# Added matmuls in the pauses of TensorE, in layer 2 of a four-layer kernel

## The chip, the cores and the metric

The kernel runs on one core of a Trainium2 chip. The metric is the device time of one execution in microseconds (us), as the median of several runs. Of the core's engines these matter here: TensorE (PE in the profile, its weight loads PEld) multiplies matrices into PSUM; VectorE (DVE) and ScalarE (ACT) work element by element; GpSimd (POOL) gathers and scatters rows by indirect DMA; SyncE (SP) issues most other DMAs.

## What is computed

`x` is 32 sequences of 64 rows of 256 float32 numbers, 2048 rows in all. Four layers follow one another, each with a mixing part and a feed-forward part, and each adds its result to `x`. The change lies in layer 2. Its mixing part is a recurrence over the 64 steps of a sequence, and its feed-forward part lets each of 8 experts choose its 512 best rows:

```python
xW = jnp.einsum('ntd,dh->nth', x, Wx) + b
def step(prev_h, xw_t):
    next_h = jnp.tanh(xw_t + prev_h @ Wh)
    return (next_h, next_h)
_, hs = jax.lax.scan(step, h0, jnp.swapaxes(xW, 0, 1))
...
k = max(MIN_CAPACITY, ceil(N * CAPACITY_FACTOR / E))
scores = jax.nn.softmax(xt @ Wr, axis=-1)
G, idx = jax.lax.top_k(scores.T, k)
X_in = xt[idx]
h = jax.nn.gelu(jnp.einsum('ekd,edh->ekh', X_in, W1) + b1[:, None, :], approximate=False)
X_e = jnp.einsum('ekh,ehd->ekd', h, W2) + b2[:, None, :]
contrib = (G[..., None] * X_e).reshape(E * k, D)
out = jnp.zeros((N, D), dtype=x.dtype).at[idx.reshape(-1)].add(contrib)
```

Here `h0` is the conditioning input, `xt` is the recurrence's output by rows, and `N` is 2048.

## The kernel before

The four layers run one after another. Layers 0 to 2 share one set of pools: `bank()` gives one of four PSUM tiles of 128x512, `wide()` one of two of 128x1024. Layer 3 opens its own PSUM pool after these are closed. The code is traced in program order; a scheduler then gives each engine its own instructions in an order, taking among those that it reckons ready the one traced first. Each engine runs its list in order, and waits on semaphores for the others. A float32 matmul shows as two records of PE and two weight loads, a transpose as one.

Layer 2 has these stages.

- **Recurrence** (`layer2`). XT holds the input transposed, HT the states transposed. `feed(s)` puts the input projection of step s into PSUM (8 matmuls through `add`, line 1111, with Wx; at every eighth step also the bias, line 1101, into a new bank). `add(s, wh, ...)` adds the product of the state before with Wh (8 matmuls, also line 1111, 16 records). ScalarE takes tanh (line 1131), VectorE transposes the new state (line 1132), and the next step's product needs that. Between them TensorE can do only what doesn't depend on the new state: `feed(s + 4)`, and at every fourth step `route(s - 1)`, two matmuls (line 1123, four records) that put the router's logits into the first 128 columns of the wide tile `lg`. Its other half, columns 512 on, isn't used. `feed` calls may run further ahead than four steps, as far as the four banks go.
- **Scores.** After the last `route`, VectorE copies the logits (line 1145), softmax follows, and TensorE transposes the scores (line 1185).
- **Search** (`top_tokens`). 15 rounds find each expert's 512th score, two bits a round. In each, VectorE counts the scores above three trial values (line 1200), one small matmul adds the counts up by expert (line 1203), and VectorE picks the next trials (lines 1207 to 1211). Then TensorE transposes the result (line 1213), and some prefix sums settle ties (lines 1223, 328 to 330).
- **Slots** (`slots`, with `by_position=True` only here). `positions` makes prefix sums with two matmuls (lines 300, 301). VectorE builds index arithmetic and, for each expert, a 128x2048 one-hot tile (line 345); TensorE multiplies it into the list of row numbers, 16 matmuls of float16 per expert (line 385). Expert 0's list goes out first, so that GpSimd can gather its rows (line 452) while the other lists are made.
- **Experts** (`routed`). For each expert, the gathered rows are transposed (line 459), the hidden layer is 16 matmuls of 128x128 by 128x512 (line 426) and the output 32 matmuls (line 435).

Of the kernel before, what the change touches and what calls it, by code (L numbers as in the profile page):

```python
# [20 lines left out]
P = 128  # L21
NB = 32
NS = 64
N = NB * NS
NT = N // P
# [4 lines left out]
NE = 8  # L30
# [40 lines left out]
class Kernel:  # L71
# [34 lines left out]
    def evacuate(self, out, in_):  # L106

        self.turn += 1
        if self.turn % 2:
            self.nc.scalar.copy(out, in_)  # L110
        else:
            self.nc.vector.tensor_copy(out, in_)

    def row_broadcast(self, pool, name, row, width, parts=P, tag=None, engine=None):

# [178 lines left out]
    def positions(self, pool, flags, ne, name):  # L294

        nc = self.nc
        off = self.scanned(pool, flags, ne, name)
        ps = self.bank()
        pos = ps[:, :ne * NT].rearrange("p (e t) -> p e t", t=NT)
        nc.tensor.matmul(pos, self.before, flags[:, :, 1:], start=True, stop=False)  # L300
        nc.tensor.matmul(pos, self.ones, off, start=False, stop=True)
        return pos

    def count_sequences(self, pool, flags):
# [43 lines left out]
    def slots(self, pool, flags, capacity, name, by_position=False):  # L348

        nc = self.nc
        nchunk = -(-capacity // P)
        full = [P, NE, NT]
        sel = flags[:, :, 1:]
        pos = self.positions(pool, flags, NE, "sl")
        other = pool.tile(full, F32, name="sl_other")
        nc.vector.tensor_scalar(other, sel, -1.0, 1.0, ALU.mult, ALU.add)

        nc.vector.scalar_tensor_tensor(other, pos, float(capacity), other, ALU.is_ge, ALU.max)  # L360
        key = pool.tile(full, I32, name="sl_key")
        nc.vector.scalar_tensor_tensor(key, other, float(N), pos, ALU.mult, ALU.add)
        part_i = pool.tile(full, I32, name="sl_part_i")
        nc.vector.tensor_scalar(part_i, key, P - 1, None, ALU.bitwise_and)
        part = pool.tile(full, F16, name="sl_part")
        nc.vector.tensor_copy(part, part_i)
        chunk = pool.tile(full, I32, name="sl_chunk")
        nc.vector.tensor_scalar(chunk, key, 7, None, ALU.logical_shift_right)

        give = pool.tile([P, NE, NT, nchunk], F16, name="sl_give")  # L370
        indices = []
        ohs = self.one_hots()

        for e0, e1 in ((0, 1), (1, NE)):
            ne = e1 - e0
            ps = self.bank()
            for c in range(nchunk):
                nc.vector.scalar_tensor_tensor(give[:, e0:e1, :, c], chunk[:, e0:e1], float(c),
                                               self.number.unsqueeze(1).to_broadcast([P, ne, NT]),
                                               ALU.is_equal, ALU.mult)  # L380
            for e in range(e0, e1):
                oh = self.one_hot(ohs, e, part)
                at = (e - e0) * nchunk
                for t in range(NT):
                    nc.tensor.matmul(ps[:, at:at + nchunk], oh[:, :, t], give[:, e, t],
                                     start=(t == 0), stop=(t == NT - 1))
            n = ne * nchunk
            read = self.cp.tile([P, n], I32, name=f"{name}_read{e0}")
            nc.scalar.activation(read, ps[:, :n], AF.Relu, bias=self.minus)  # L389
            add = self.cp.tile([P, n], I32, name=f"{name}_add{e0}")  # L390
            if by_position:

                nc.vector.tensor_scalar(add, read, NB - 1, NS.bit_length() - 1, ALU.bitwise_and,
                                        ALU.logical_shift_left)
                nc.vector.scalar_tensor_tensor(add, read, NB.bit_length() - 1, add, ALU.logical_shift_right,
                                               ALU.bitwise_or)
                empty = pool.tile([P, n], I32, name=f"sl_empty{e0}")
                nc.vector.tensor_scalar(empty, ps[:, :n], 0.5, self.spare, ALU.is_lt, ALU.mult)
                nc.vector.tensor_tensor(add, add, empty, ALU.bitwise_or)
            else:  # L400
                empty = pool.tile([P, n], F32, name=f"sl_empty{e0}")
                nc.vector.tensor_scalar(empty, ps[:, :n], 0.5, self.spare1, ALU.is_lt, ALU.mult)
                nc.vector.scalar_tensor_tensor(add, ps[:, :n], -1.0, empty, ALU.add, ALU.add)
            indices += [(read[:, i:i + 1], add[:, i:i + 1]) for i in range(n)]
        return indices, nchunk
# [663 lines left out]
    def layer2(self, weights):  # L1069
        nc, tc, I = self.nc, self.tc, self.I  # L1070
# [3 lines left out]
        XT = self.xp.tile([P, DC, NS, NB], F32, name="XT", tag="XT")  # L1074
        both = P // NS
        for t in range(NT):
            ps = self.bank()
# [6 lines left out]
        HT = self.xp.tile([P, DC, NS, NB], F32, name="HT", tag="CT")  # L1084
# [5 lines left out]
        with tc.tile_pool(name="l2r", bufs=1) as rp:  # L1090
            wx, wh, b, ones, wr = weights
            width = DC * NB
            steps = 512 // width
            into = {}

            def feed(s):

                if s % steps == 0:
                    into[s // steps] = ps = self.bank()
                    for q in range(QG):  # L1100
                        nc.tensor.matmul(
                            ps[q * NB:(q + 1) * NB].rearrange("p (s x) -> p s x", x=width), ones,
                            b[:, q].rearrange("p m f -> p (m f)").unsqueeze(1).to_broadcast([3 * NB, steps, width]),
                            start=True, stop=True)
                add(s, wx, lambda c: XT[:, c, s])

            def add(s, w, state):
                at = s % steps * width
                for c in range(DC):
                    for q in range(QG):  # L1110
                        nc.tensor.matmul(into[s // steps][q * NB:(q + 1) * NB, at:at + width], state(c),  # L1111
                                         w[:, c, q].rearrange("p m f -> p (m f)"), start=False,
                                         stop=True, skip_group_check=True)

            lead = 4
            lg = self.wide()
            rows = table[:, :D].rearrange("(s b) d -> b s d", b=NB)

            def route(s):

                t = s // 4
                for c in range(DC):
                    nc.tensor.matmul(lg[:, t * NE:(t + 1) * NE], HT[:, c, s - 3:s + 1].rearrange("p s b -> p (s b)"),  # L1123
                                     wr[:, c], start=(c == 0), stop=(c == DC - 1))

            for s in range(lead):
                feed(s)
            for s in range(NS):
                add(s, wh, lambda c: self.condT[:, c, :] if s == 0 else HT[:, c, s - 1])
                at = s % steps * width  # L1130
                nc.scalar.activation(H[:, s], into[s // steps][:, at:at + width], AF.Tanh)
                nc.vector.transpose(HT[:, :, s], H[:, s].rearrange("p (m f) -> p m f", f=NB))
                if s % 4 == 0 and s:
                    route(s - 1)
                if s + lead < NS:
                    feed(s + lead)
                if s % 16 == 15:
                    for q in range(QG):
                        for m in range(DC):
                            f = m * P + q * NB  # L1140
                            nc.sync.dma_start(rows[:, s - 15:s + 1, f:f + NB],
                                              H[q * NB:(q + 1) * NB, s - 15:s + 1, m * NB:(m + 1) * NB])
            route(NS - 1)
            logits = rp.tile([P, NT, NE], F32, name="r2_l")
            nc.vector.tensor_copy(logits.rearrange("p t e -> p (t e)"), lg[:, :NT * NE])
            score = rp.tile([P, NT, NE], F32, name="score")
            self.softmax(rp, score, logits, [P, NT, NE])
            nc.scalar.dma_start(table[:, D:].rearrange("(t p) e -> p t e", p=P), score)
            k = max(4, math.ceil(N * 2.0 / NE))
            self.top_tokens(rp, flags, score, k)  # L1150
# [8 lines left out]
    def top_tokens(self, pool, flags, scores, k):  # L1159
# [6 lines left out]
        m = 2  # L1166
# [31 lines left out]
        for i, shift in enumerate(shifts):  # L1198
# [1 line left out]
                nc.vector.tensor_scalar(seen, by, trial.bitcast(F32)[:, j:j + 1], 0.0, ALU.is_ge, ALU.add,  # L1200
                                        accum_out=cnt[:, j:j + 1])
            ps = self.bank()
            nc.tensor.matmul(ps[:, :J], members, cnt, start=True, stop=True)
            more = i + 1 < len(shifts)
            if more:
                nc.vector.tensor_tensor(base, tries[:, i + 1], kth.to_broadcast([P, J]), ALU.bitwise_or)
# [754 lines left out]
```

## Time and profile before

| | us |
|---|---|
| median of 3 runs | 1902.01 (1901.94 to 1907.29) |
| the profiled execution, its own time | 1906.38 |
| its span, first to last instruction | 1904.7 |
| mean granted TensorE clock over the span | 0.866 of full speed |
| recurrence, first tanh to last | 942.57 to 1029.71 |
| scores, last `route` to the transpose of line 1185 | 1030.27 to 1033.66 |
| search, first count to the transpose of line 1213 | 1035.75 to 1070.72 |
| slots, from there to the first expert's line 426 | 1070.72 to 1096.27 |

A time in the profile is in us from the span's start. A group line gives the engine, its line in the kernel, the operation, the tile written and the tiles read, how often, and in brackets how long the engine stood idle before and who ended that. The granted clock is the share of full speed at which TensorE was let run; a stage's mean can lie between the steps of 0.5 and 1.0 that single stretches show.

### The profile page before, as it was taken

How to read it: one execution, taken by the hardware profiler on the slowest of the kernel's cores; microseconds unless marked ns; L12 is line 12 of the kernel's file. 1: busy time of each engine (PE TensorE's matmuls, PEld its weight loads, DVE VectorE, ACT ScalarE, POOL GpSimd, SP SyncE). 2: the span in 40 equal slices, each digit the busy share in tenths (PEclk: the TensorE clock that was granted, in tenths of full speed). 3: DMA queues.
4: the chain of work that ended last, by engine and by line, in shares of the span. 5: the costliest groups of instructions: out<-in, count | busy, mean ns of one | idle time of the engine just before them, and what ended most of it. 6: DMA issues, size and time to landing. Idle time of an engine off the chain costs nothing.

```text
span 1904.7 us, 26705 instructions
## 1 busy us (share of the span) xinstructions
PE 1548.1 (81%) x9935; PEld 1193.5 (63%) x9935; DVE 713.6 (37%) x2357; ACT 599.6 (31%) x1306; POOL 576.0 (30%) x740
## 2 busy tenths in 40 slices
PE   6699998999996939999675499999665768778777
PEld 5467766888885728888564356667543546546455
DVE  3594033111111161111213601001356668787775
ACT  2222332333331203333211032222134455545443
POOL 0244310233320013332100133331235445555452
PEclk8699998999997959999885599999866778788789
DMA  7454541566632045666511044442300100101000
GB/s 255 125 167 129 141 122 59 162 182 181 190 96 88 6 157 158 191 177 169 150 26 25 12 117 127 106 112 64 114 31 22 41 22 23 32 14 32 14 12 12
DMA packets 158406, 183.81 MB, mean 97 GB/s; under 512 B 37540, under 2 KB 137536, under 8 KB 158272
## 3 DMA queue, kind: packets, MB, share of 16 engines
q1 hardware_dynamic: 123920, 143.34, 23.7%
q0 software_dynamic: 21248, 29.24, 8.9%
q10 hardware_dynamic: 13104, 9.47, 1.6%
q8 instruction: 81, 1.33, 0.3%
q14 instruction: 53, 0.43, 0.1%
HBM read 152.22 MB, written 29.79 MB: 96 GB/s over the span
## 4 chain that ended last, share of the span: by engine, by line
PE 27%; DVE 8%; POOL 6%; issue 5%; ACT 4%; DMA 1%; SPq 0%; POOLq 0%; DVEq 0%; ACTq 0%
PE bank L426 6%; PE bank L435 6%; PE bank L1111 3%; PE bank L1740 2%; PE bank L1856 2%; PE bank L1663 1%; PE bank L1873 1%; PE bank L1437 1%; ACT squares L1582 1%; PE bank L1798 1%; PE bank L1575 1%; POOL mag L1332 1%; PE wide L1123 1%; PE bank L1774 1%; POOL mb_root L147 1%
## 5 line engine op out<-in xcount | busy, mean ns | idle before, releaser
L435 PE MATMUL bank<-w,hidden 128*128 128x256 f32 (+1 forms) x2080 | 458.7, 379 | 0.0
L435 PEld LDWEIGHTS bank<-w,hidden 128*128 128x128 f32 (+1 forms) x2080 | 387.8, 187 | 66.2 <-issue 6.5
L426 PE MATMUL bank<-xeT,w 128*128 128x256 f32 (+2 forms) x1440 | 398.5, 436 | 25.9 <-ACT xeT L110 20.5
L426 PEld LDWEIGHTS bank<-xeT,w 128*128 128x128 f32 x1440 | 274.7, 193 | 137.1 <-issue 63.4
L469 POOL DMA_INDIRECT acc<-y,l_add x56 | 89.2, 1594 | 254.8 <-ACT y L468 146.1
L603 DVE TENSOR_TENSOR y<-bank,b 128x256 f32<-128x256 f32 x58 | 24.6, 425 | 360.8 <-PE bank L435 360.8
L428 ACT ACTIVATE hidden<-bank,ge_cols 128x256 f32<-128x256 f32 x232 | 109.8, 473 | 114.9 <-PE bank L426 114.9
L452 POOL DMA_INDIRECT xg<-table,l_read x56 | 71.7, 1280 | 244.9 <-ACT l_read L389 164.9
L467 DVE TENSOR_TENSOR y<-bank,b 128x256 f32<-128x256 f32 (+1 forms) x56 | 23.5, 420 | 297.7 <-PE bank L435 297.6
L428 ACT ACTIVATE hidden<-bank,bias_cols_b 128x256 f32<-128x256 f32 (+1 forms) x128 | 73.7, 580 | 120.6 <-PE bank L426 119.6
L605 POOL DMA_INDIRECT acc_c<-y,pl_add x30 | 47.8, 1594 | 137.0 <-DVE gate L595 98.6
L605 POOL DMA_INDIRECT acc<-y,pl_add x28 | 44.6, 1592 | 131.7 <-DVE gate L595 93.5
L1856 PE MATMUL bank<-wg,yT 128*128 128x352 f32 x128 | 58.2, 586 | 15.3 <-ACT h_glu L1858 7.2
L1663 PE MATMUL bank<-wqkv,mo_uT 128*128 128x512 f32 (+1 forms) x128 | 57.2, 602 | 15.9 <-ACT ex L1727 13.3
L468 ACT ACTIVATE y<-y,xg 128x256 f32<-128x256 f32 (+1 forms) x56 | 28.4, 508 | 128.7 <-DVE y L467 128.7
L1873 PE MATMUL bank<-wd,hT 128*128 128x256 f32 x192 | 62.1, 465 | 6.1 <-ACT hT L1577 2.9
L426 PE MATMUL bank<-XT,w 128*128 128x256 f32 x256 | 65.0, 409 | 2.0 <-DVE C L899 1.3
L110 ACT COPY xeT<-bank 128x256 f32<-128x256 f32 (+1 forms) x57 | 20.6, 362 | 143.7 <-PE bank L124 88.0
L604 ACT ACTIVATE y<-y,gate 128x256 f32<-128x256 f32 x58 | 29.5, 509 | 106.9 <-DVE y L603 106.9
L1856 PE MATMUL bank<-wu,yT 128*128 128x352 f32 x128 | 54.0, 546 | 9.9 <-DVE h_glu L1860 9.1
L591 POOL DMA_INDIRECT xg<-table_x,pl_read x30 | 31.9, 1062 | 99.1 <-DVE pl_empty L544 57.5
L426 PEld LDWEIGHTS bank<-XT,w 128*128 128x128 f32 x256 | 51.0, 205 | 9.6 <-DVE C L899 1.4
(581 smaller groups left out, 2391.6 us busy)
## 6 DMA issues: line engine op xcount, KB each, us to landing
w<-in_L_ffn_W_dram SPq DMA_DIRECT2D x44, 1024.0 KB
w<-in_L_cond_ew_dram SPq DMA_DIRECT2D x30, 1024.0 KB
w<-in_L_ffn_w_dram SPq DMA_DIRECT2D x16, 1024.0 KB
ad<-ada SPq DMA_DIRECT2D x64, 128.0 KB
X<-acc SPq DMA_DIRECT2D x12, 512.0 KB
w<-in_L_cond_sw_dram SPq DMA_DIRECT2D x4, 1024.0 KB
ad<-ada SPq DMA_DIRECT2D x64, 64.0 KB
b<-in_L_ffn_b_dram SPq DMA_DIRECT2D x30, 128.0 KB
```

Source lines behind the costliest of these rows:

```text
L426: nc.tensor.matmul(ps[:, :cols], w1[:, c, f * P:(f + 1) * P], xT[:, c, :], start=(c == 0), stop=(c == DC - 1))
L428: nc.scalar.activation(h[:, f, :cols], ps[:, :cols], func, bias=bias[:, f:f + 1])
L435: self.nc.tensor.matmul(ps[:rows, :D], h[:, f, at:at + rows], w2[:, f, :], start=(f == 0), stop=(f == FC - 1))
L452: nc.gpsimd.indirect_dma_start(out=xg[:rows], out_offset=None, in_=table, in_offset=bass.IndirectOffsetOnAxis(ap=indices[e * nchunk + c][0 ...
L469: nc.gpsimd.indirect_dma_start(out=acc, out_offset=bass.IndirectOffsetOnAxis(ap=indices[e * nchunk + c][1][:rows], axis=0), in_=y[:rows], ...
L591: nc.gpsimd.indirect_dma_start(out=xg, out_offset=None, in_=table, in_offset=bass.IndirectOffsetOnAxis(ap=read[:, c:c + 1], axis=0), bound ...
L605: nc.gpsimd.indirect_dma_start(out=acc, out_offset=bass.IndirectOffsetOnAxis(ap=add[:, c:c + 1], axis=0), in_=y, in_offset=None, bounds_ch ...
L1111: nc.tensor.matmul(into[s // steps][q * NB:(q + 1) * NB, at:at + width], state(c), w[:, c, q].rearrange("p m f -> p (m f)"), start=False, ...
L1663: nc.tensor.matmul(ps[:, :hi - lo], uT[:, j, c], K["wqkv"][:, c, lo:hi], start=(c == 0), stop=(c == DC - 1))
L1740: nc.tensor.matmul(ps[rows, h * (HD + 1):(h + 1) * (HD + 1)], ex[rows, r, j * DC + c, odd], V[rows, j, h], start=True, stop=True)
L1856: nc.tensor.matmul(ps[:, :half], yT[:, c], w[:, c, cols], start=(c == 0), stop=(c == DC - 1))
L1873: nc.tensor.matmul(ps[:, :D], hT[:rows, k], self.wd[:rows, k], start=(k == 0), stop=(k == KC - 1))
```

## The change

A new helper, `repeat`, issues n float32 matmuls of the identity (128x128) with the first `width` columns of XT into the unused half of `lg`, which nothing reads. `issue_after(mark)` puts them behind a given instruction in TensorE's order; they wait for nothing else. It is called with width 128 once per step of the recurrence, and with width 512 otherwise: 5 after the last `route`, 3 after each of the 15 counts, 4 after the slots' prefix sums, 3 after expert 0's one-hot products and 1 after each of experts 1, 2 and 3. That is 64 matmuls of 128 columns and 60 of 512. The computed result doesn't depend on them.

```diff
+    def repeat(self, mark, n, width=P):
+
+        with self.tc.issue_after(mark):
+            for _ in range(n):
+                self.nc.tensor.matmul(self.unread[:, :width], self.ident, self.any_rows[:, :width], start=True,
+                                      stop=True)
+
...
-        nc.tensor.matmul(pos, self.ones, off, start=False, stop=True)
+        self.last_count = nc.tensor.matmul(pos, self.ones, off, start=False, stop=True).ins
...
         pos = self.positions(pool, flags, NE, "sl")
+        if by_position:
+            self.repeat(self.last_count, 4, 512)
...
-                    nc.tensor.matmul(ps[:, at:at + nchunk], oh[:, :, t], give[:, e, t],
-                                     start=(t == 0), stop=(t == NT - 1))
+                    last = nc.tensor.matmul(ps[:, at:at + nchunk], oh[:, :, t], give[:, e, t],
+                                            start=(t == 0), stop=(t == NT - 1))
+                if by_position and e < 4:
+                    self.repeat(last.ins, 1 if e else 3, 512)
...
             lg = self.wide()
+            self.unread = lg[:, 512:]
+            self.any_rows = XT.rearrange("p c s b -> p (c s b)")
...
-                add(s, wh, lambda c: self.condT[:, c, :] if s == 0 else HT[:, c, s - 1])
+                mark = add(s, wh, lambda c: self.condT[:, c, :] if s == 0 else HT[:, c, s - 1])
...
                 if s + lead < NS:
                     feed(s + lead)
+                self.repeat(mark, 1)
...
-            route(NS - 1)
+            self.repeat(route(NS - 1), 5, 512)
...
-            nc.tensor.matmul(ps[:, :J], members, cnt, start=True, stop=True)
+            self.repeat(nc.tensor.matmul(ps[:, :J], members, cnt, start=True, stop=True).ins, 3, 512)
```

`add` and `route` return their last matmul for this.

## The prediction

> **What bounds the kernel now.** I read the page first, then busy time by stage, then stretches of 3.41 us, then single instructions in order of time.
>
> ```profile
> PE 1548.1 (81%) x9935; PEld 1193.5 (63%) x9935; DVE 713.6 (37%) x2357; ACT 599.6 (31%) x1306; POOL 576.0 (30%) x740
> ...
> PEclk8699998999997959999885599999866778788789
> ```
>
> TensorE carries most of the span. A slice of the second line is 47.6 us; slices 21 and 22, counted from 0 (1000 to 1095 us), have half the clock. They are the end of layer 2's recurrence, its search and its slots. Busy time in those stages (columns: PE, PEld, DVE, ACT, POOL, granted clock, DMA share, GB/s):
>
> ```profile
> 942.57:1029.93 87.36, 65.50 (x2047) 53.47 (x2039) 15.45 (x63) 14.28 (x64) 0.00 (x0) 0.74 0.22 50
> 1034.50:1070.40 35.90, 8.73 (x30) 7.51 (x30) 23.90 (x176) 0.00 (x0) 0.00 (x0) 0.50 0.05 5
> 1076.53:1079.24 2.71, 0.00 (x1) 0.00 (x1) 2.60 (x11) 0.00 (x0) 0.00 (x0) 0.50 0.00 0
> 1079.24:1096.27 17.03, 10.73 (x137) 9.57 (x137) 10.30 (x17) 1.01 (x3) 7.05 (x4) 0.50 0.12 33
> ```
>
> They are the recurrence, the 15 rounds of the search, the pause after the slots' prefix sums, and the one-hot products. The clock is 0.74 in the first and 0.50 in the rest. In stretches of 3.41 us:
>
> ```profile
> 992.27:995.68 3.41, 2.66 (x118) 2.17 (x106) 0.74 (x3) 0.67 (x3) 0.00 (x0) 1.00 0.06 11
> 995.68:999.10 3.42, 2.12 (x79) 1.55 (x68) 0.74 (x3) 0.67 (x3) 0.00 (x0) 0.98 0.00 0
> 999.10:1002.51 3.41, 2.44 (x76) 1.96 (x80) 0.73 (x3) 0.67 (x3) 0.00 (x0) 0.50 0.02 5
> ```
>
> A stretch with 79 matmul records is followed by half clock; one with 118 is not. So filling does matter here. What a step costs is seen in the distance between ScalarE's tanh's (full clock, then half clock, steps without a projection):
>
> ```profile
> 995.87 0.22 ACT L1131 ACTIVATE H<-bank 128x64 f32<-128x64 f32 x1 [0.83 <-PE bank L1111]
> 996.93 0.22 ACT L1131 ACTIVATE H<-bank 128x64 f32<-128x64 f32 x1 [0.83 <-PE bank L1111]
> ...
> 1006.20 0.22 ACT L1131 ACTIVATE H<-bank 128x64 f32<-128x64 f32 x1 [1.06 <-PE bank L1111]
> 1007.48 0.22 ACT L1131 ACTIVATE H<-bank 128x64 f32<-128x64 f32 x1 [1.05 <-PE bank L1111]
> ```
>
> 1.06 against 1.28 us: half clock costs 0.22 us a step. One round of the search, at half clock:
>
> ```profile
> 1043.08 0.59 PE L1203 MATMUL bank<-tk_cnt,tk_members 128*128 128x3 f32 x2 [1.81 <-DVE tk_seen L1200]
> 1043.71 0.16 DVE L1207 TENSOR_SCALAR_CACHE_REDUCE tk_enough<-bank 128x3 f32<-128x3 f32 x1 [0.68 <-PE bank L1203]
> ...
> 1045.48 0.59 PE L1203 MATMUL bank<-tk_cnt,tk_members 128*128 128x3 f32 x2 [1.81 <-DVE tk_seen L1200]
> ```
>
> The period is 2.40 us, of which TensorE works 0.59 and pauses 1.81; VectorE bounds it. The price of a repeated matmul, from the chain of work of a later expert:
>
> ```profile
> 1128.10 13.97 PE bank L426 x32
> ```
>
> That line is 16 matmuls of 128x128 by 128x512 in float32, each in two records (32): 13.97/16 = 0.873 us each at clock 1.00. The added ones have this very shape and type.
>
> **The change, part by part.** It removes nothing, moves no DMA, and touches neither SP's nor POOL's queue. It adds matmuls on TensorE, which runs them in order; each stands behind a named matmul and waits for nothing. What is queued behind them on TensorE is the next recurrent product, the next count L1203, the transposes L1185 and L1213, and the one-hot products L385; VectorE and ScalarE wait for all of these. The extra hold on XT and on lg's second half costs nothing: no later tile uses either name, and the PSUM pool is closed only at layer 3, after the last repeat. That cover would be gone only if layer 3 came before the slots.
>
> 1. Recurrence, 64 repeats of 128x128 by 128x128: a quarter of 0.873 us, so 0.21 each at full clock, 0.43 at half. The gain first: steps 8 to 24, nearly all at full clock, took 956.04 to 976.43 = 20.4 us, 10.2 for eight steps. Steps 8 to 63 took 73.7 us (956.04 to 1029.71); at 10.2 for eight they'd take 70.1, saving 3.6. Steps 2 to 8, partly at half clock, save about 1.3. Together 4.9. The cost: the 16 recurrent records take 0.27 us to issue, so a step of 1.06 leaves 0.79; two input projections (0.28 each) and a repeat fill 0.77, so the repeat hides. In the 16 steps that also hold the router's four records (0.54 us) TensorE is the bound already (0.54+0.56+0.27 = 1.37, and 956.04 to 957.41 is 1.37), so 16 x 0.21 = 3.4 is added. Net -1.5. Bounds: -4.9 (router steps find room) and +4 (the clock still drops, and a repeat costs 0.43 where it doesn't fit).
> 2. After the last router product, 5 repeats of 512: 5 x 0.873 = 4.37. L1185 starts 3.39 us after that product starts (1030.27, 1033.66) because of softmax. After: 0.54 + 4.37 = 4.91, so +1.5; the transpose's own 0.15 is saved: +1.35. If the clock is half at first, up to +4.5.
> 3. Search, 3 repeats in each of 15 rounds. 3 x 0.873 = 2.62 us must pass through a pause of 1.81. The count itself at full clock is 0.27 (two records at 0.135, a quarter of the router's 0.54), and the first repeat's weights load after it, about 0.06 to 0.13. The period is 2.62+0.27+0.06 = 2.95 us, bound by TensorE. The last round's repeats also stand before L1213. From the first count to L1213 it was 34.97 us (1035.75 to 1070.72); it becomes 15 x 2.95 = 44.3: +9.3. Bounds: +8.4 at 2.89 a round, +10.3 at 3.02. That the count gets 0.26 faster is in the 2.95 and buys nothing beyond.
> 4. L1213 to the second prefix sum's end, 5.81 us with 3.82 of PE at half clock: at most half of that, 1.9, is saved if the clock stays, and I reckon 1.5, since what follows the last column of each doesn't shrink; PE is busy under half the time there, like the stretches that dropped. I take -0.8 (0 to -1.5).
> 5. 4 repeats behind the prefix sums: 3.49 us at full clock, 6.98 at half, in a pause of 2.71. +0.8 to +4.3; the clock may have dropped in part 4 and must be won back: +1.9.
> 6. Slots' one-hot products: 3 repeats behind expert 0's, 1 behind each of experts 1 to 3. The first 16 records take 1.16 and gain 0.3 to 0.5, an estimate with half of it as its limit. Those after experts 0 to 2 lie in the wait for the gathers (TensorE idles for L459 until 1090.83). The one behind expert 3 does not: after 1090.83 TensorE works without a pause up to the first expert's L426. +0.9 to +1.75 there. If full clock lasted to 1091, the other products would gain 2.5. Net +1.2 (-3 to +3). The first L426 run took 16.36 us against 13.97, 2.4 lost to half clock; a wait of over 5 us for gathers precedes it still, so I leave it at 0 (±2.4).
>
> Sum: -1.5 +1.35 +9.3 -0.8 +1.9 +1.2 = +11.5 us. The profiled execution took 1906.4 us (span 1904.7 and 1.7 around it), 4.4 above the median of 1902.0; I put the same sum on both: 1917.9 for a profiled one, 1913.5 for the median.
>
> Two rules of the Trainium skill bear on this, both on the page TensorE: Matmul & The Clock Gate. The section Back-to-back issue gap gives a warm 512-column matmul about 216 ns. By that, three repeats are 0.65 us and vanish in 1.81; the search would only gain, about 15 x 0.26 = 3.9. By the row they are 2.62. The row has the shape and the float32 of this edit, so it decides. The section Why this matters for your kernels asks only for no idle gap above about 3 us to stay warm. By that, the search, with pauses of 1.8, would be at full clock already and the repeats could buy nothing: without the gains of parts 1 and 4 the sum is about +17. The rows speak against it: 0.50 all through the search.
>
> **Rivals.**
> - Repeats fit and clock gains remain (faster). The place is the search; it is decided by a 512 repeat costing at most 0.6 us (a round without repeats is 2.40-0.26 = 2.14 at full clock, less 0.3 for the count, by 3). Then: recurrence -4.9, counts -3.9, part 4 -1.5, one-hots -2.5, first L426 -2.4: -15, 1887 us. The clock rows speak for it, the 0.873 against. 0.08.
> - Balance (within 0.3%): search as reckoned, but router steps take the repeat for nothing (-4.9), and the slots stay at full clock to 1091 with the first L426 (-3.6, -2.4): near +1 to +4, 1904 us. For it: TensorE will be full for 45 us before. Against: the waits for gathers. 0.18.
> - Repeats cost and the clock doesn't hold in the recurrence and slots (slower still): +4, +4.5, +9.3, +4.3, +3 = +25, 1927 us. For it: 79 records were too few, and steps without projections get only two more records. Against: those two stream four times the columns of eight small ones. 0.10.
> - TensorE becomes the bound of the search and the rest about cancels: 1913.5 us. 0.64.
>
> **How the numbers follow.** About 0.3%, 5.7 us, is what a measurement of this kernel can tell from no change. Most of the likeliest case and all of the third lie above 1907.7: slower 0.73; balance and the low edge of the likeliest: same 0.19; faster 0.08. The range 1901 to 1923 takes in the balance and leaves out the first rival and the outer part of the third. The likeliest case's own range is 1907 to 1921.
>
> **What would show it.** In the profile after: 3 repeats as 6 records between counts, the period 2.9 to 3.0 us, PE near 100% busy with clock 1.00 there, and VectorE's L1200 no longer what the count waits for. L1185 starts about 4.9 us after the last router product, L1213 44 us after the first count. In the recurrence the clock is near 1.0 and tanh's are 1.06 apart, about 1.58 at router steps. It is wrong if a 512 repeat takes under 0.6 us, if the search's round is below 2.4, or if the recurrence shrinks by more than 5.

## The result, and the profile after

The changed kernel took 1908.34 us in the median of 12 runs (1904.01 to 1913.79), the kernel before 1904.10 in 12 runs beside it (1901.73 to 1910.35): ratio 1.0026, 95% interval 1.0016 to 1.0036. So it is slower by 4 to 5 us, clear of the noise but less than half of the 11.5 that were forecast. 1908.3 lies in the range of 1901 to 1923. The difference of 0.26% is inside the 0.3% that the prediction called no change, to which it gave 0.19, against 0.73 for slower.

The profiled execution took 1906.77 us with a span of 1905.0, the same as before (1904.7). That is chance: the first tanh of layer 2 came at 939.41 us instead of 942.57, after code that is the same in both, and in all 13 traces of this study it came between 938.8 and 945.4. So I compare stages, not spans. In the changed kernel L118 is the repeat; the recurrence's L1111 has become L1122, the router's L1123 is L1137, the logits' copy is L1161, the count L1219, the one-hot products L394, the gathered rows' transposes L470 and the hidden layer L437.

| stage, from start to start | before | after | change | forecast |
|---|---|---|---|---|
| recurrence, first tanh to last | 87.14 | 79.69 | -7.45 | -1.5 |
| last tanh to the first count | 6.07 | 9.90 | +3.83 | +1.35 |
| search, to the transpose of its result | 34.94 | 43.75 | +8.81 | +9.3 |
| to the first one-hot products | 8.52 | 7.99 | -0.53 | +1.1 |
| to the first expert's hidden layer | 17.03 | 15.03 | -2.00 | +1.2 |
| that hidden layer | 16.34 | 16.74 | +0.40 | 0 |
| sum | | | +3.06 | +11.45 |

Busy time by stage after the change (the columns as in the prediction): recurrence, search, and one-hot products.

```profile
939.41:1019.32 79.91, 75.18 (x2179) 60.32 (x2179) 15.47 (x63) 14.28 (x64) 0.00 (x0) 0.98 0.25 58
1029.00:1072.75 43.75, 43.75 (x121) 21.07 (x121) 23.09 (x171) 0.00 (x0) 0.00 (x0) 0.96 0.00 1
1080.74:1095.77 15.03, 15.03 (x150) 11.89 (x148) 9.78 (x15) 1.01 (x3) 6.18 (x4) 0.86 0.15 38
```

The clock went from 0.74 to 0.98 in the recurrence and from 0.50 to 0.96 in the search. But in the search TensorE is now busy all of the time. One round there, in order of time:

```profile
1064.35 0.28 PE L1219 MATMUL bank<-tk_cnt,tk_members 128*128 128x3 f32 x2
...
1064.49 2.82 PE L118 MATMUL wide<-XT,ident 128*128 128x512 f32 x6
1064.67 0.16 DVE L1223 TENSOR_SCALAR_CACHE_REDUCE tk_enough<-bank 128x3 f32<-128x3 f32 x1 [1.07 <-PE bank L1219]
...
1066.31 0.08 DVE L1216 DVE_READ_ACCUMULATOR tk_seen<-tk_by,tk_try 128x1 f32 x1
...
1067.15 0.28 PE L1219 MATMUL bank<-tk_cnt,tk_members 128*128 128x3 f32 x2
```

The period is 2.80 us, 2.40 before; the six records of the repeats take 2.66 of it (1064.49 to 1067.15). VectorE has finished its counts at 1066.39; the count matmul starts at 1067.15, without any wait of its own, because three repeats run ahead of it. VectorE is the one that waits now, 1.07 us a round.

The stage of the scores holds what I had not foreseen:

```profile
1019.65 0.61 PE L1137 MATMUL wide<-r_w,HT 128*128 128x8 f32 x4 [0.20 <-DVE HT L1147]
...
1020.12 4.54 PE L118 MATMUL wide<-XT,ident 128*128 128x512 f32 x10
...
1024.70 0.29 DVE L1161 COPY r_l<-wide 128x128 f32<-128x128 f32 x1 [5.10 <-PE wide L118]
```

The copy of the logits doesn't start when the router's last product ends (1020.26), but when the five repeats end (1024.66). Softmax then begins 4.4 us late, and the repeats are over before the pause that they were to fill.

### The profile page after: what moved, and what is told of

It is laid out like the page before. It is cut to its first block, busy times and chain, and to the rows that moved or that the text cites. A ratio compares the mean times of both kernels' runs of the same rounds, so it can differ in the third digit from the quotient of the medians.

```text
span 1905.0 us, 27201 instructions
## 1 busy us (share of the span) xinstructions
PE 1598.9 (84%) x10183; PEld 1214.8 (64%) x10183; DVE 714.2 (37%) x2357; ACT 599.6 (31%) x1306; POOL 576.0 (30%) x740
## 4 chain that ended last, share of the span: by engine, by line
PE 30%; DVE 9%; POOL 6%; ACT 4%; issue 2%; DMA 1%; SPq 0%; POOLq 0%; DVEq 0%; ACTq 0%
PE bank L437 6%; PE bank L446 6%; PE wide L118 4%; PE bank L1756 2%; PE bank L1872 2%; PE bank L1122 2%; PE bank L1679 1%; PE bank L1889 1%; PE bank L1453 1%; ACT squares L1598 1%; PE bank L1814 1%; PE bank L1591 1%; POOL mag L1348 1%; PE bank L1790 1%; POOL mb_root L154 1%
## 5 line engine op out<-in xcount | busy, mean ns | idle before, releaser
L437 PE MATMUL bank<-xeT,w 128*128 128x256 f32 (+2 forms) x1440 | 397.2, 435 | 25.8 <-ACT xeT L110 21.3
L437 PEld LDWEIGHTS bank<-xeT,w 128*128 128x128 f32 x1440 | 273.9, 193 | 136.5 <-issue 61.7
L118 PE MATMUL wide<-XT,ident 128*128 128x128 f32 (+1 forms) x248 | 89.5, 471 | 0.0
L437 PE MATMUL bank<-XT,w 128*128 128x256 f32 x256 | 64.2, 405 | 2.0 <-DVE C L910 1.4
```

The source lines that it names most:

```text
L118: self.nc.tensor.matmul(self.unread[:, :width], self.ident, self.any_rows[:, :width], start=True, stop=True)
L437: nc.tensor.matmul(ps[:, :cols], w1[:, c, f * P:(f + 1) * P], xT[:, c, :], start=(c == 0), stop=(c == DC - 1))
```

## The experiments

My theory after seeing this: the repeats buy the clock, worth about 7 us in the recurrence; three in a round of the search are one too many, and the five after the router hold back the copy because they write the same tile. Rivals are named with each run. Every kernel was timed beside the kernel before on the same chip; the stage times are from its one trace.

### rec_only: the recurrence's repeats alone

```diff
         pos = self.positions(pool, flags, NE, "sl")
-        if by_position:
-            self.repeat(self.last_count, 4, 512)
...
-                if by_position and e < 4:
-                    self.repeat(last.ins, 1 if e else 3, 512)
...
-            self.repeat(route(NS - 1), 5, 512)
+            route(NS - 1)
...
-            self.repeat(nc.tensor.matmul(ps[:, :J], members, cnt, start=True, stop=True).ins, 3, 512)
+            nc.tensor.matmul(ps[:, :J], members, cnt, start=True, stop=True)
```

> The change's repeats in the recurrence alone (64 of 128 columns); none elsewhere. Theory (the recurrence gains from the clock and the other stages give it back): first tanh to last about 80 us as in the changed kernel (79.7) against 87.1 before, granted clock there near 1.0; scores, search and slots as before; total 6 to 7.5 us below before. Rival (the 79.7 was this one trace's luck): 84 to 88 us and a total within 2 us of before.

Measured: 1896.97 us, ratio 0.9946 (0.9927 to 0.9966), 8 us below before by the medians, a little more than expected. Recurrence 80.97 us at clock 0.96, search 34.94 and one-hot products 17.03 as before. Busy time in its recurrence:

```profile
945.00:1025.97 80.97, 76.38 (x2178) 61.20 (x2179) 15.46 (x63) 14.12 (x64) 0.00 (x0) 0.96 0.24 54
```

The gain is real, and the other stages give it back. Over the six traces that share this recurrence, changed kernel included, it took 79.7 to 82.0 us, so the 7.45 of the table is the best of a spread of 5.1 to 7.5. The spread lies in the start: steps 8 to 63 took 65.1 to 65.7 in all six, the first eight 14.0 to 16.6. Before, the first eight took 13.5, and 15.4 in the trace of slots_order below, whose recurrence is the old one. So the repeats gained nothing in the first eight.

### rec_narrow: the same repeats, 8 columns wide

```diff
-                self.repeat(mark, 1)
+                self.repeat(mark, 1, 8)
```

(on rec_only)

> As rec_only, but each of the 64 repeats has 8 columns instead of 128: the same number of added instructions, nearly none of the streaming. Theory (streamed columns keep the clock up): clock in the recurrence 0.7 to 0.8, first tanh to last 86 to 89 us, total no faster than before. Rival (any matmul in the pause is enough): clock near 1.0 and about 78 us, since the repeat itself costs less.

Measured: 1925.43 us, ratio 1.0095 (1.0076 to 1.0114). It is 20 us slower, far outside what either theory said. Busy time in the recurrence of this kernel:

```profile
944.79:1054.90 110.11, 104.81 (x2179) 91.76 (x2179) 15.45 (x63) 14.22 (x64) 0.00 (x0) 0.58 0.17 39
```

Matmuls are in flight 95% of the time (104.81 of 110.11) and the clock is 0.58, the lowest of all the recurrences here; in rec_only they were in flight 94% of the time (76.38 of 80.97), at 0.96. So busy time in the records is not what holds the clock. That the streamed columns do is what the theory said, and it fits, but the width also changed the scheduler's order of the projections. The order alone doesn't hold the clock either (rec_even, below, 0.75). A narrow repeat is not cheap, as its step at half clock, in order of time, shows:

```profile
983.80 0.65 PE L1118 MATMUL bank<-Wh,HT 128*32 128x64 f32 x16
...
984.39 0.50 PEld L118 LDWEIGHTS wide<-XT,ident 128*128 128x128 f32 x2 [0.17 <-issue]
984.39 0.60 PE L118 MATMUL wide<-XT,ident 128*128 128x8 f32 x2
...
984.54 0.22 ACT L1142 ACTIVATE H<-bank 128x64 f32<-128x64 f32 x1 [1.78 <-PE bank L1118]
...
984.91 0.84 PEld L1118 LDWEIGHTS bank<-Wx,XT 128*32 128x32 f32 x32
```

The two loads of 128x128 weights take 0.50 us, then two whole projections (32 records) follow before the next recurrent product, and a step is 1.97 us long (984.54 to 986.51) where before 1.28 or 1.43 was usual at half clock. Here the loads cost time and bought no clock.

### rec_even: no repeats, the projections spread evenly

```diff
-                add(s, wh, lambda c: self.condT[:, c, :] if s == 0 else HT[:, c, s - 1])
+                mark = add(s, wh, lambda c: self.condT[:, c, :] if s == 0 else HT[:, c, s - 1])
...
                 if s + lead < NS:
-                    feed(s + lead)
+                    with tc.issue_after(mark):
+                        feed(s + lead)
```

(on the kernel before)

> No repeats at all; the input projection of step s+4 is put behind step s's recurrent product in TensorE's order, so that each pause holds one projection instead of two in some and none in others. It computes the same. Theory (the clock comes from the added columns): with 16 small records in each pause TensorE is busy about as much as before on average, clock 0.6 to 0.9, 83 to 88 us, total -4 to +1. Rival (the repeats work by spreading the projections, which the order of the changed kernel also shows): clock near 1.0, 74 to 78 us, total 9 to 13 us below before.

Measured: 1897.97 us, ratio 0.9958 (0.9943 to 0.9973). Busy time in its recurrence, first tanh to last plus the last state's transpose:

```profile
944.17:1027.30 83.13, 64.47 (x2056) 51.34 (x2056) 15.45 (x63) 14.18 (x64) 0.00 (x0) 0.75 0.23 53
```

The clock is that of before (0.75 against 0.74), as the theory had it, yet the stage is at 82.99 us, 4.15 below before, at the low end of what the theory allowed. The median is 7 below, more than the theory's 4. So the even order is a gain of its own, without the clock. Where it comes from is not shown. In the kernel before, the scheduler put two projections (32 records) into some pauses and none into others, but at full clock both kinds of step took 1.05 to 1.06 us, router steps aside. What differs between the two traces is waits of TensorE for nothing visible ("issue"). The kernel before has one of 3.61 near its start and three more:

```profile
959.40 0.25 PE L1111 MATMUL bank<-Wx,XT 128*32 128x64 f32 x3 [0.85 <-issue]
...
963.40 0.48 PE L1111 MATMUL bank<-Wx,XT 128*32 128x64 f32 x20 [0.80 <-issue]
...
971.41 0.43 PE L1111 MATMUL bank<-Wh,HT 128*32 128x64 f32 x15 [0.73 <-issue]
```

rec_even has one of 2.20 near its start and no other. The difference, 3.8 us, is nearly all of the 4.15. Whether the order removes such waits is open, since traces of the same recurrence differ in them too: slots_order has one of 3.85 and one of 0.44 (steps 8 to 63 took 73.67 us before and 72.03 there, and without the waits 71.3 and 71.6). The changed kernel has one of 2.92 and one of 0.29. The repeats change the order too: most pauses of the changed kernel hold 14 to 24 projection records, where before many held none and some 32 or more.

### own_tile: the repeats write a tile of their own

```diff
-            self.unread = lg[:, 512:]
+            self.unread = self.wide()[:, 512:]
```

(on the changed kernel)

> The changed kernel, but the repeats write into the second half of a wide tile of their own instead of the unused half of the logits' tile. Theory (the copy of the logits waits for the five repeats because they write the tile that it reads): the copy starts about 1.1 us after the last router product's start instead of 5.05, and last tanh to the transpose of the scores falls from 7.96 to about 5.3, then set by the repeats ahead of the transpose; total 2.5 us below the changed kernel. Rival (the copy is held by TensorE's order of work, not by the tile): 7.9 to 8.0 us, no difference.

Measured: 1904.55 us, ratio to before 0.9998 (0.9987 to 1.0010), some 4 below the changed kernel. Last tanh to the scores' transpose is 5.40, and the copy starts behind the router. TensorE in order of time:

```profile
1023.98 0.61 PE L1137 MATMUL wide<-r_w,HT 128*128 128x8 f32 x4 [0.20 <-DVE HT L1147]
1024.44 4.54 PE L118 MATMUL wide<-XT,ident 128*128 128x512 f32 x10
```

The copy on VectorE, while those repeats still run:

```profile
1024.63 0.29 DVE L1161 COPY r_l<-wide 128x128 f32<-128x128 f32 x1 [0.70 <-PE wide L1137]
```

The wait came from the shared tile, although the columns don't overlap. The search fell as well, from 43.75 to 42.05: 15 rounds of 2.80 us, all at full clock. In the changed kernel the clock was down in the first rounds (0.62 from 1030.81 to 1034.22), after the pause that had opened in softmax, and the first repeats were slow.

### two, one and short: how many repeats the search and the scores take

On own_tile: two has 2 repeats after a count instead of 3, one has 1; short has 2 after a count and 2 instead of 5 behind the router.

> As own_tile (the changed kernel with the repeats in a tile of their own), but 2 repeats after each count of the search instead of 3. Theory (three fill more than the round has: 6 records of 0.43 and 0.22 for the count are the 2.80 us period that was measured): the period falls to VectorE's chain at full clock, 2.13 to 2.17 us, with the clock still 1.0 there; first count to the transpose falls from 42.05 to about 32 (34.94 before the change), total 10 us below own_tile. Rival (the round is slow for the traffic of the repeats, or two don't hold the clock): 2.4 us or more a round, 35 us or more.

> As two, but 1 repeat of 512 columns after each count. It tells how much streaming holds the clock: 0.87 us of columns in a round of about 2.15. If the clock stays at 1.0, first count to the transpose is 31 to 32 us, as with two; if it drops, a repeat costs 1.7 us at half clock, which still fits, and the round is 2.40 as before the change: 34.5 to 35.5 us. My theory says it drops, since 40% of the time is less than the stretches of the recurrence had that dropped (79 records).

> As two, and 2 repeats instead of 5 after the last router product. Theory (five delay the transpose of the scores, two end before softmax does): last tanh to that transpose falls from 5.40 to about 3.6 us, the clock holds into the search; total 1.5 to 2 us below two. Rival (with two the clock drops in softmax and the first rounds of the search are slow): 3.6 to 4.0 there, and 1 to 3 us more in the search, no gain.

Measured: two 1896.84 us (0.9957; 0.9942 to 0.9973), one 1897.35 (0.9952; 0.9933 to 0.9971), short 1891.16 (0.9921; 0.9896 to 0.9945). Search of two: 32.93 us at clock 1.00, the period 2.20 us. TensorE in order of time:

```profile
1045.58 0.38 PE L1219 MATMUL bank<-tk_cnt,tk_members 128*128 128x3 f32 x2
1045.82 1.96 PE L118 MATMUL wide<-XT,ident 128*128 128x512 f32 x4
1047.78 0.38 PE L1219 MATMUL bank<-tk_cnt,tk_members 128*128 128x3 f32 x2
```

So it is the third repeat that costs: 42.05 less 32.93 is 9.1 us for 15 of them (7.7 of it in the median, 10 expected). With one repeat the search took 33.30, and my theory was half wrong: the clock neither held nor stayed down, but changed from stretch to stretch. Busy time in one's search, the clock third from the end:

```profile
1044.89:1048.31 3.42, 2.09 (x7) 1.04 (x8) 2.29 (x19) 0.00 (x0) 0.00 (x0) 1.00 0.00 0
1048.31:1051.72 3.41, 1.96 (x6) 0.52 (x4) 2.76 (x21) 0.00 (x0) 0.00 (x0) 1.00 0.00 0
1051.72:1055.13 3.41, 3.16 (x7) 1.69 (x8) 1.94 (x16) 0.00 (x0) 0.00 (x0) 0.54 0.01 2
1055.13:1058.55 3.42, 3.42 (x6) 1.09 (x5) 2.57 (x21) 0.00 (x0) 0.00 (x0) 0.50 0.02 5
1058.55:1061.96 3.41, 2.50 (x8) 1.04 (x8) 2.28 (x17) 0.00 (x0) 0.00 (x0) 0.96 0.00 0
```

A drop at 1052 is won back at 1058.8; while the clock is down a repeat takes twice as long and fills the stretch. The pauses at full clock were short, as TensorE just before that drop shows:

```profile
1049.77 0.39 PE L1219 MATMUL bank<-tk_cnt,tk_members 128*128 128x3 f32 x2 [0.85 <-DVE tk_seen L1216]
1050.01 1.10 PE L118 MATMUL wide<-XT,ident 128*128 128x512 f32 x2
1051.97 0.59 PE L1219 MATMUL bank<-tk_cnt,tk_members 128*128 128x3 f32 x2 [0.85 <-DVE tk_seen L1216]
```

Short took 4.48 in the scores, not the 3.6 expected, since the clock was down there in its trace (0.63), but still less than two's 5.40, or the 7.10 of one, whose clock fell as its five repeats began; its search took 32.94, no more than two's. It gained 5.7 us on two in the median. In the two traces 0.9 is in the scores, 0.9 in the slots and 2.9 in the first hidden layer, where its clock was full from the start; that phase of the clock differs from trace to trace, so how much of the 5.7 the edit made is not placed.

### both: even projections and repeats together

```diff
                 if s + lead < NS:
-                    feed(s + lead)
-                self.repeat(mark, 1)
+                    with tc.issue_after(mark):
+                        feed(s + lead)
+                if s % 4 or not s:
+                    self.repeat(mark, 1)
```

(on short)

> As short, and the input projections in the even order of rec_even, with a repeat in every step but the 16 that hold a router product. Theory (the even order and the clock are separate gains: the order ends the long steps where two projections share a pause, the repeats keep the clock): first tanh to last about 73 to 76 us against 80 to 82 with repeats alone and 83.0 with the even order alone, clock near 1.0; total 5 to 7 us below short. Rival (they are one gain): 79 to 81 us.

Measured: 1888.44 us, ratio 0.9909 (0.9886 to 0.9932), 17 us below before and the fastest form here with lean and no_slots. Busy time in all but the ends of its recurrence:

```profile
945.00:1018.00 73.00, 69.91 (x2116) 55.49 (x2116) 15.20 (x62) 13.68 (x62) 0.00 (x0) 0.95 0.24 54
```

First tanh to last is 74.56 us. Beside rec_even that is 8.4 us less for the clock, beside short 7.0 less for the order and the spared repeats at router steps, which no run tells apart: two gains. The median fell by 2.7 only. In the two traces, 3.5 us of the 7.0 are given back between the search and the end of the first hidden layer (39.5 us against 36.0 in short), where the clock was 0.81 and 0.87 at first instead of 1.00.

### slots_order, lean and no_slots: what the slots gained from

Before, the one-hot products of experts 3 to 5 stood behind the first of the gathered rows' transposes (L459), which wait for GpSimd's gathers. TensorE in the kernel before, in order of time:

```profile
1084.44 1.13 PE L385 MATMUL bank<-sl_give,oh 128*128 128x4 f16 x16
1086.27 0.69 PE L459 MATMUL bank<-ident,xg 128*128 128x128 f32 x2 [0.71 <-DMA xg<-table,l_read]
1088.47 0.69 PE L459 MATMUL bank<-ident,xg 128*128 128x128 f32 x2 [1.51 <-DMA xg<-table,l_read]
1090.83 0.44 PE L459 MATMUL bank<-ident,xg 128*128 128x128 f32 x1 [1.67 <-DMA xg<-table,l_read]
1091.07 1.14 PE L385 MATMUL bank<-sl_give,oh 128*128 128x4 f16 x16
```

In the changed kernel they stand ahead of these transposes (L470):

```profile
1088.16 1.11 PE L394 MATMUL bank<-sl_give,oh 128*128 128x4 f16 x16
...
1090.07 2.09 PE L394 MATMUL bank<-sl_give,oh 128*128 128x4 f16 x32
1092.02 1.31 PE L470 MATMUL bank<-ident,xg 128*128 128x128 f32 x5
```

slots_order sets that order without any repeat:

```diff
+                    behind = tc.issue_after(self.hots) if name == "l2f" and e == 0 else ExitStack()
+                    with behind:
+                        for d in range(DC):
+                            nc.tensor.transpose(ps[:, d * P:d * P + rows], xg[:rows, d * P:(d + 1) * P],
+                                                self.ident[:rows, :rows])
```

(on the kernel before; `self.hots` is the last one-hot product of expert 5)

> The kernel before, without any repeat; only in the slots, the transposes of expert 0's gathered rows are put behind the one-hot products of expert 5 in TensorE's order (they stood behind those of expert 2). It computes the same. Theory (the slots' gain of 2.0 us came because the repeats made the scheduler place those transposes later, so that the wait for the gathers no longer holds back experts 3 to 5): from expert 0's one-hot products to the first L426, 17.03 before and 15.03 after the change, it takes 14.2 to 15.2 us at clock 0.50; total 1.5 to 3 us below before. Rival (the gain is the full clock): 16.8 to 17.2 us.

Measured: 1901.28 us, ratio 0.9988 (0.9981 to 0.9995). From the first one-hot products to the first expert's hidden layer it took 14.08 us at clock 0.50, 17.03 before at the same clock. TensorE in order of time:

```profile
1078.81 5.76 PE L385 MATMUL bank<-sl_give,oh 128*128 128x4 f16 x80 [1.96 <-DVE oh L345]
1084.43 1.52 PE L463 MATMUL bank<-ident,xg 128*128 128x128 f32 x6
1087.35 0.66 PE L463 MATMUL bank<-ident,xg 128*128 128x128 f32 x2 [1.39 <-DMA xg<-table,l_read]
1087.80 2.11 PE L385 MATMUL bank<-sl_give,oh 128*128 128x4 f16 x32
```

The order alone gives more than the repeats did (15.03). Two more, on both: lean has this order, 3 repeats behind the prefix sums and none behind the one-hot products; no_slots has none in the slots at all.

> As both, but 3 repeats behind the prefix sums instead of 4, none behind the one-hot products, and the transposes in the order of slots_order. Theory (once the order is set the slots' repeats buy only what the clock gives there, some 0.1 us in 16 records): first prefix repeat ends before the one-hot tile is ready, prefix sums to one-hots falls to 7.3 to 7.6 from 8.0 where the clock is full, one-hot products to L426 15 us; total within 2 us of both. Rival (without them the clock is at half in the first expert's L426 for longer): 1 to 3 us more than both.

> As lean, and without the repeats behind the prefix sums, so that the slots have none at all. Theory (there a repeat is only in the way: at half clock three take 5.2 us in a pause of 2.7, at full clock the stage gains 0.6): from the transpose of the search's result to the first one-hot products 7.9 to 8.5 us, at either clock, against 9.94 in lean and 9.16 in both; from there to L426 14 to 14.2; total 0 to 2 us below lean. Rival (the repeats keep the clock for the prefix sums and the first expert): 8.5 us and a slower first L426, 1 us or more above lean.

Measured: lean 1888.36 us (0.9918; 0.9905 to 0.9931), no_slots 1889.24 (0.9903; 0.9886 to 0.9919). From the search's transpose to the first one-hot products: 9.94 in lean, whose clock had dropped there (0.66), 7.74 in no_slots (0.75), 7.98 in short, with four repeats at clock 1.00. From there to the first hidden layer both took 14.06, at clock 0.62 and 0.50. So in these traces a repeat in the slots cost time where the clock was down, and the stage was no faster for the clock. The totals of the two can't be told from both's. Their searches, though with two repeats, took 34.3 and 34.2 us, not 32.9: the clock was down in the first rounds (0.95 over the search).

## Why the prediction was right and where it failed

The side held, and so did the mechanism of the largest term: TensorE became the bound of the search, because a 512-column float32 repeat takes what the row had said. That 43.75 us came so near to the forecast of 44.3 is in part luck. A round took 2.80 us, not 2.95: the count and the first repeat's weights took 0.14 (1064.35 to 1064.49), not 0.33. At full clock throughout that makes 42.05, as in own_tile; the slow first rounds put 1.7 back. That the total fell into the range is in good part luck too. The likeliest case's own range, 1907 to 1921, holds the time at its edge, but the recurrence alone was 6 us off, and the prediction's own sign of being wrong, a recurrence that shrinks by more than 5, came true in all six traces. Four more steps failed, three of them in the change's favour.

- **Part 1, recurrence: -1.5 forecast, -7.45 in the trace, -5.1 to -7.5 over six.** The failed term is the gain, 4.9. The prediction took 10.2 us for eight steps as the price at full clock, but the 16 steps behind that held the three waits for nothing visible shown under rec_even, 2.4 us together. Without them eight steps are 9.0, and steps 8 to 63 would gain 11.8 instead of 3.6; less the 3.4 for router steps that is 8.4, and 7.95 was measured (73.67 to 65.72; 6.3 from slots_order's 72.03, which has fewer waits). So the waits went into the price of a step, and the gain was too small by what they add up to over 55 steps. Why the waits come in some traces and not in others stays open. The 1.3 us reckoned for steps 2 to 8 did not come: the first eight took 0.5 longer than before. The cost at router steps was right in kind: most are 1.45 to 1.6 apart in the trace, 1.58 by the text, 1.37 before.
- **Part 2, scores: +1.35 forecast, +3.83 measured.** The failed step is the sentence that the repeats wait for nothing and that only the transpose stands behind them. VectorE's copy waited for all five through the shared tile (own_tile: 7.96 to 5.40). What the prediction described, 4.9 us to the transpose, is what own_tile measured: 1023.98 to 1028.82, 4.84.
- **Parts 4 and 5, prefix sums and the repeats behind them: +1.1 forecast, -0.53 measured.** Part 4 gained 1.1, 0.8 forecast. In part 5 the failed term is the allowance for a clock that has dropped: it was still 1.00, so the four repeats took 3.44 us (1077.30 to 1080.74), near the 3.49 of the text, and the pause grew by 0.6 instead of 1.9.
- **Part 6, slots: +1.2 forecast, -2.00 measured.** The failed step is "The one behind expert 3 does not". It took the order of the one-hot products and transposes as fixed, and the repeats changed it. That order, not the clock, is the gain: slots_order gained 2.95 without repeats and at clock 0.50.

One of the prediction's smaller counts doesn't come out: if the "eight small ones" are projection records, they stream 8 x 64 columns, and the two of a repeat 2 x 128, half as many and not four times.

The rule of the Trainium skill that the prediction weighed (page TensorE: Matmul & The Clock Gate, section Why this matters for your kernels) lets a pause be as long as about 3 us. The prediction held the 0.50 of the old search against it. That is no test: the same section asks for about 4 us of continuous work before the clock is full, and in the kernel before the clock had fallen at 1029.7, before the search began. The run with one repeat is a test. It was at full clock, paused 0.85 us a round and lost the clock at 1052 all the same, so the runs decide against the rule as the only condition.

Of the rivals, "balance" (1904) came nearer to the measured time than the likeliest case (1913.5): its gains in recurrence and slots are there, though not for its reasons. "The clock doesn't hold" was refuted by 0.98 in the recurrence.

## What to carry to other kernels

Filling TensorE's pauses to keep its clock can pay (8.4 us of 83 in the recurrence, 0.7 to 2.0 of 34.9 in the search), but count the filler in records of its own shape and type against the pause at full clock: one too many turned -2.0 into +7.1 (own_tile). Give it a tile that nothing reads, and look at what it does to the scheduler's order: the order alone took 7 us off the median in the recurrence (rec_even) and 3 us off the slots (slots_order). When a price is read from a stretch of the trace, first look for waits in it that have nothing to do with the price. Judge a change by stages, as single traces start this layer up to 6.7 us apart.

## What the runs showed of the hardware

- TensorE was in flight 95% of the time at clock 0.58 (rec_narrow), and 94% at 0.96 (rec_only). Weight loads with 8 columns behind them did not hold the clock. A 128x8 float32 repeat took 0.50 us at half clock for its two loads.
- In the search, six records of 128x512 float32 took 2.66 us at full clock, 0.44 each.
- In the trace of one, from 1020 to 1073, the clock changed at about 1021.2, 1024.6, 1031.5, 1038.3, 1052.0, 1058.8, 1065.6 and 1072.4. The distances are whole multiples of 3.41 us. In the stretch that ends at 1052.0 the repeats streamed for about 1.0 us and the clock was lost; in the three before it they streamed for 1.2 us or more, and it was kept. These are estimates, from the starts of the repeats and 0.43 us a record, in one trace.
- VectorE's read of one half of a PSUM tile waited 4.4 us for TensorE's writes to the other half; with a second tile it did not. Whether the chip needs that wait, or only the program's semaphores ask for it, was not tried.
